# One group of small products instead of two, and a new order of a turn's parts, in the layers of a transformer on one core

## The chip, the cores and the metric

The kernel runs on one core of one Trainium2 chip. A core has five engines that matter here. TensorE (PE in the profile, PEld its weight loads) multiplies matrices, from on-chip memory into eight accumulation banks. VectorE (DVE), ScalarE (ACT) and GpSimd (POOL) do elementwise work; SyncE (SP) issues the transfers. Each engine runs its own list of instructions strictly in order, and waits, through semaphores, for what an instruction needs from other engines. So the order in which the program lists instructions on each engine decides what stands behind what.

The metric is the time of one execution on the device, in microseconds (us).

## The reference

The input x has 2 sequences of 1024 tokens with 128 features. Eight blocks follow one another, each of them adding to x: windowed attention, an expert network, causal attention, the expert network again, an attention with 16 heads, then `L1_ffn`, another attention, and `L1_ffn` once more. The change touches `L1_ffn` alone, which runs twice. It has six layers:

```python
for i in range(DEPTH):                                    # 6
    x = attn_layer(shift_tokens(x), Wqkv[i], q_scale[i], k_scale[i], Wo[i]) + x
    x = ffn_layer(shift_tokens(x), ln_g[i], ln_b[i], W1[i], b1[i], W2[i], b2[i]) + x
```

`attn_layer` makes queries, keys and values for 16 heads of 64 numbers, scales queries and keys to length one (`l2norm`), rotates them by position, and lets each window of 32 tokens attend to itself and to the window before: products of queries and keys, a mask, a softmax, products with the values, and a projection back to 128 features. `ffn_layer` normalises each token, makes 2 x 341 numbers of it, multiplies one half by the gelu of the other, and goes back to 128 features.

## The kernel before, in words

Class `Layers` works on tiles of 128 tokens (four windows). A layer has 2 x 8 tiles, a call 6 x 16 = 96, numbered m. The tile stays in on-chip memory from layer to layer. The work on one tile is cut into some 70 steps, each a method of the class that issues a few instructions. The attention steps come once a tile, the `ffn_...`, `gate...` and `value...` steps (the list `BY_BLOCK`) once in four tiles, on 512 tokens at a time.

The steps are software-pipelined by hand. `ORDER` is a list of words such as `scores0:0`; `turns` goes through it once a turn, and in turn n the word `step:late` runs that step for tile m = n - late. So a step with late -3 works three tiles ahead of one with late 0. The place in the list sets the order in which the instructions of one turn stand on each engine's list; nothing rearranges them afterwards (`manual_schedule`). A call has 110 turns, the first ones and the last ones only partly filled.

A tile passes through these steps. The numbers after a step's name are its arguments; for queries and keys the first is s (0 queries, 1 keys), the second the half u.

- `project` s u (L1448, PE): queries or keys of 128 tokens, 512 columns, into one bank of the pool `pj` (four banks).
- `squares` s u (L1457, ACT) reads that bank and squares it; `rotate` s u (L1477, DVE) reads the same bank and multiplies by the rotary table into `t1` and `t2`, of which there are two buffers each.
- `halves` s (L1483, POOL) adds the two halves of the squares; `lengths` s (L1489, DVE) sums them per head; `inverses` (L1502 to L1504, ACT) makes one over the root.
- `join` s (L1494, POOL) adds `t1` and `t2` into `raw`; `scale` s (L1509, POOL) multiplies `raw` by the inverse lengths.
- `flip` s c (L201, PE, tile `tqk`): four transposes into one of two banks of tag `tp`; `heads` s c (L1527, ACT) copies them out. `carry` (L1542, POOL) hands the last keys on to the next tile.
- `project_v` r (L1550, PE), `values` r (L1559, ACT), `windows` r (L1567 to L1574, SP): values, and eight transfers that lay them out by window.
- `scores` (L1588 and L1597, PE): eight mask matmuls and 64 small products, of 64 x 32 by 64 columns, which PE runs several at a time in parts of its array. The profile counts each product as two matmuls, for a float32 product takes two passes. `below_max` j (DVE), `exps` j (ACT) and `sums` (DVE) are the softmax.
- `flip_p` j (PE, tile `tpr`), `probabilities` j (ACT); `outputs` (L1647, PE): 64 small products again; `divide` r (DVE).
- `flip_o` r (PE, tile `to`), `features` r (ACT), `project_out` (L1679, PE: 16 matmuls in the profile), `add_out` (DVE).
- for four tiles: `ffn_flip`, `ffn_stats`, `ffn_dev`, `ffn_norm`, `ffn_back`, `ffn_gain`, three `gate_in` and `gate`, three `value_in` and `value`, `ffn_out` (L1789), `ffn_add`.

Before, `scores` and `outputs` each come in two parts, `scores0` and `scores1`, `outputs0` and `outputs1`, with half of the small products each (64 matmuls of the profile), and other PE work between the parts. Weights and rotary tables are fetched inside `project`, `rotate` and `ffn_add`, whichever of a layer's calls comes first.

Of the kernel before, what the change touches and what calls it, by code (L numbers as in the profile page):

```python
# [11 lines left out]
F32 = mybir.dt.float32  # L12
# [6 lines left out]
P = 128  # L19
# [11 lines left out]
DEPTH, LH, LD, LW = 6, 16, 64, 32  # L31
# [1019 lines left out]
class Experts:  # L1051
# [223 lines left out]


ORDER = """
    value_in1:11 halves0:-2 join0:-2 add_out:3 flip11:0 divide0:2 divide1:2 project_v0:0 ffn_flip:7
    heads01:0 flip_p0:1 gate_in0:9 heads11:0 value_in0:11 lengths1:-1 value1:11 value_in2:10 values0:0
    scores0:0 lengths0:-2 inverses:-1 project10:-2 ffn_back:8 flip_p1:1 ffn_stats:7 gate0:9 value0:11  # L1280
    ffn_out:11 ffn_dev:7 squares10:-2 sums:1 ffn_norm:7 project11:-2 carry:0 project00:-3 value2:10
    rotate10:-2 scores1:0 probabilities0:1 squares11:-2 project_v1:0 ffn_gain:8 probabilities1:1
    flip_o0:2 scale1:-1 ffn_add:11 gate_in2:9 flip_o1:2 windows0:0 rotate11:-2 squares00:-3 values1:0
    scale0:-1 gate_in1:9 rotate00:-3 features0:2 features1:2 below_max0:0 halves1:-2 gate2:9
    below_max1:0 project01:-3 flip10:-1 gate1:9 squares01:-3 exps0:0 outputs0:1 join1:-2 heads10:-1
    rotate01:-3 project_out:2 flip00:-1 heads00:-1 exps1:0 outputs1:1 flip01:-1 windows1:0
"""
BY_BLOCK = (
    "ffn_flip", "ffn_stats", "ffn_dev", "ffn_norm", "ffn_back", "ffn_gain", "gate_in", "gate",
# [4 lines left out]
class Layers:  # L1294
# [281 lines left out]

    def scores(self, m, part):
        nc, st = self.nc, self.get(m)  # L1580
        key = self.name(m)
        if part == 0:
            st["sc"] = [self.ps.tile([P, 8, 64], F32, tag="big", name=f"sc_{key}_{j}") for j in range(2)]
            first = self.place(m)[2] == 0
            for c in range(4):
                for j in range(2):
                    rows = slice(64 * j, 64 * j + 64)
                    nc.tensor.matmul(  # L1588
                        st["sc"][j][ts(c, 32)].rearrange("p h k -> p (h k)"), self.identb[rows, :],
                        self.wide[rows, 1 if first and c == 0 else 0, :], start=True, stop=False,  # L1590
                    )
        sc = st["sc"]
        for hp in range(4 * part, 4 * part + 4):
            for c in range(4):
                for j in range(2):
                    rows = slice(64 * j, 64 * j + 64)
                    nc.tensor.matmul(  # L1597
                        sc[j][ts(c, 32), hp, :], st["q"][rows, hp, ts(c, 32)],
                        st["k"][rows, hp, ds(32 * c, 64)], start=False, stop=(hp == 7),
                    )  # L1600
# [33 lines left out]
        pt = st["pT", j] = self.sp.tile([P, 4, P], F32, tag="pT", name=f"pT_{self.name(m)}_{j}", bufs=4)  # L1634
        self.nc.scalar.copy(pt, st["tpr", j])

    def outputs(self, m, part):
        nc, st, key = self.nc, self.get(m), self.name(m)
        if part == 0:
            st["av"] = [self.pj.tile([P, 4, 2, LD], F32, tag="pj", name=f"av_{key}_{r}") for r in range(2)]  # L1640
        av = st["av"]
        for q in range(2 * part, 2 * part + 2):
            for j in range(2):
                for c in range(4):
                    for r in range(2):
                        rows = slice(64 * r, 64 * r + 64)
                        nc.tensor.matmul(  # L1647
                            av[r][ts(c, 32), q, j, :], st["pT", j][rows, q, ts(c, 32)],
                            st["vw"][rows, c, ts(2 * q + j, LD)], start=True, stop=True,
                        )  # L1650
# [318 lines left out]
```

## Time and profile before

| | |
|---|---|
| median of three runs | 3995.49 us (3991.46 to 3996.87) |
| the profiled execution: its span | 3987.0 us |
| the median less that span | 8.5 us |
| PE busy | 3825.6 us, 96% of the span |
| DVE, ACT, POOL busy | 3116.1, 2414.0, 2535.5 us |
| mean granted clock of PE | 0.970 |
| first call of `Layers` | about 563 to 2225 us of the span |
| second call of `Layers` | about 2311 to 3973 us |
| longest waits of ACT and POOL | ACT on flips of queries 387.8, on projections 367.6; POOL on squares 308.7 us |
| PE's wait for `scale` (tqk on raw, L1509) | 13.9 us |

The profile is one execution of the program. The profiled execution's own time is known as its span, from the first to the last instruction; what a run takes beyond it is the difference in the table. A row of a group gives the line, engine, operation, output and inputs with their shapes and count, then after the bar the busy time in us and the mean length of one in ns, and after the second bar the engine's idle time just before, with what ended it. A row of a timeline gives the start and the length in us, and in brackets the idle time before it. Matmuls overlap, so on PE the difference between two starts says more than a length. The chain of work that ended last lies on PE for 87% of the span.

### The profile page before, as it was taken

The numbers are of one execution on the slowest core, as the hardware profiler recorded it, in microseconds if no ns is written. First come the engines' busy times: TensorE is split into PE (matmuls) and PEld (weight loads), VectorE is DVE, ScalarE is ACT, GpSimd is POOL, SyncE is SP. The second block draws the span as 40 slices with busy tenths as digits, with TensorE's granted clock in tenths as the row PEclk, the third lists the DMA queues.
The fourth block names the chain that finished last, engine by engine and source line by source line (L and its number), as shares of the span: only waits on it lengthen the run. The fifth ranks groups of instructions, "written<-read, shape, count | busy, mean of one in ns | idle before, by whom it ended". The sixth has DMA issues, their size and how long they took to land.

```text
span 3987.0 us, 156275 instructions
## 1 busy us (share of the span) xinstructions
PE 3825.6 (96%) x67372; PEld 2521.5 (63%) x67372; DVE 3116.1 (78%) x6012; ACT 2414.0 (61%) x4582; POOL 2535.5 (64%) x1638
## 2 busy tenths in 40 slices
PE   7898979999999999999999779999999999999998
PEld 5646436666666666666666446666666666666665
DVE  7775877778787878787887667887878787878786
ACT  3444437766666666666666458666666666666665
POOL 4541448776766667767675467766767767666662
PEclk8899979999999999999999779999999999999999
DMA  3030313232333333323222033333333323332222
GB/s 87 2 85 8 79 62 75 67 92 69 78 84 75 78 78 73 88 72 77 63 70 67 9 95 70 75 85 75 86 71 73 92 68 77 85 76 67 66 68 54
DMA packets 217397, 281.11 MB, mean 71 GB/s; under 512 B 52493, under 2 KB 108682, under 8 KB 216586
## 3 DMA queue, kind: packets, MB, share of 16 engines
q1 hardware_dynamic: 216714, 271.12, 27.9%
q8 instruction: 536, 8.78, 1.0%
q14 instruction: 147, 1.20, 0.1%
HBM read 69.46 MB, written 3.28 MB: 18 GB/s over the span
## 4 chain that ended last, share of the span: by engine, by line
PE 87%; DVE 6%; DMA 2%; POOL 2%; ACT 1%; issue 1%; SPq 0%; DVEq 0%; POOLq 0%; ACTq 0%
PE pj_l L1448 17%; PE y_l L1679 9%; PE pv_l L1550 9%; PE tqk_l L201 9%; PE av_l L1647 8%; PE sc_l L1597 7%; PE tpr_l L201 4%; PE to_l L201 4%; PE fg_l L1753 3%; PE fy_l L1789 3%; PE fa_l L1774 3%; PE sc_l L1588 2%; DMA f0share_e<-f0d_e 1%; PE f0S_e L1239 1%; DVE t_l L1477 1%
## 5 line engine op out<-in xcount | busy, mean ns | idle before, releaser
L1477 DVE TENSOR_TENSOR t_l<-pj_l,rot_l 128x512 f32<-128x512 f32 x1536 | 968.1, 684 | 368.6 <-ACT sq_l L1457 356.6
L1494 POOL TENSOR_TENSOR raw_l<-t_l,t_l 128x1024 f32<-128x1024 f32 x384 | 907.8, 2364 | 532.5 <-DVE on_l L1655 285.0
L1448 PE MATMUL pj_l<-wqkv_l,x_l 128*128 128x512 f32 x1536 | 785.9, 614 | 6.5 <-DVE t_l L1477 4.2
L1509 POOL TENSOR_TENSOR raw_l<-raw_l,rn_l 128x1024 f32<-128x1024 f32 x384 | 723.2, 1902 | 94.6 <-ACT rn_l L1504 87.4
L1483 POOL TENSOR_TENSOR sq_l<-sq_l 128x512 f32<-128x512 f32 x384 | 490.8, 1278 | 311.8 <-ACT sq_l L1457 308.7
L1457 ACT ACTIVATE sq_l<-pj_l 128x512 f32<-128x512 f32 x768 | 461.5, 603 | 369.6 <-PE pj_l L1448 367.6
L201 PE MATMUL tqk_l<-ident_sb,raw_l 128*128 128x128 f32 x3072 | 452.7, 278 | 15.5 <-POOL raw_l L1509 13.9
L1527 ACT COPY qT_l<-tqk_l 128x512 f32<-128x512 f32 x384 | 224.8, 585 | 387.9 <-PE tqk_l L201 387.8
L201 PEld LDWEIGHTS tqk_l<-ident_sb,raw_l 128*128 128x128 f32 x3072 | 356.4, 142 | 160.7 <-issue 121.3
L1550 PE MATMUL pv_l<-wqkv_l,x_l 128*128 128x512 f32 x768 | 416.4, 624 | 6.1 <-DVE ln_xn_fl L1733 5.3
L1679 PE MATMUL y_l<-outT_l,wo_l 128*128 128x128 f32 x3072 | 393.7, 281 | 0.0
L1597 PEld LDWEIGHTS sc_l<-kT_l,qT_l 64*32 64x32 f32 x24576 | 295.4, 105 | 155.5 <-issue 145.1
L1679 PEld LDWEIGHTS y_l<-outT_l,wo_l 128*128 128x128 f32 x3072 | 357.5, 191 | 18.3 <-issue 1.0
L1448 PEld LDWEIGHTS pj_l<-wqkv_l,x_l 128*128 128x128 f32 x1536 | 256.3, 192 | 172.1 <-issue 111.2
L1647 PE MATMUL av_l<-vw_l,pT_l 64*32 64x64 f32 x24576 | 360.5, 224 | 2.1 <-issue 1.7
L1559 ACT COPY v_l<-pv_l 128x512 f32<-128x512 f32 x384 | 225.1, 586 | 225.4 <-PE pv_l L1550 205.5
L1655 DVE TENSOR_TENSOR on_l<-av_l,inv_l 128x512 f32<-128x512 f32 x384 | 247.4, 686 | 121.5 <-PE av_l L1647 121.3
L1647 PEld LDWEIGHTS av_l<-vw_l,pT_l 64*32 64x32 f32 x24576 | 294.2, 105 | 70.0 <-issue 63.6
L1597 PE MATMUL sc_l<-kT_l,qT_l 64*32 64x64 f32 x24576 | 329.8, 223 | 0.3 <-issue 0.3
L201 PEld LDWEIGHTS tpr_l<-ident_sb,pr_l 128*128 128x128 f32 x1536 | 189.1, 141 | 152.3 <-issue 116.8
L1607 DVE TENSOR_TENSOR pr_l<-sc_l,mx_l 128x512 f32<-128x512 f32 x384 | 265.6, 692 | 13.2
L201 PEld LDWEIGHTS to_l<-ident_sb,on_l 128*128 128x128 f32 x1536 | 183.2, 141 | 128.4 <-issue 110.9
(317 smaller groups left out, 6208.9 us busy)
## 6 DMA issues: line engine op xcount, KB each, us to landing
vw_l<-v_l SPq DMA_DIRECT2D x3024, 64.0 KB
wqkv_l<-in_Wqkv SPq DMA_DIRECT2D x36, 512.0 KB
f0share_e<-f0d_e SPq DMA_DIRECT2D x64, 256.0 KB
rot_l<-in_rotary SPq DMA_DIRECT2D x24, 512.0 KB
wo_l<-in_Wo SPq DMA_DIRECT2D x12, 512.0 KB
w_l<-in_W SPq DMA_DIRECT2D x12, 341.0 KB
a0rows<-a0both SPq DMA_DIRECT2D x4, 512.0 KB
a0qk<-a0rows SPq DMA_DIRECT2D x32, 64.0 KB
```

The lines of the kernel that those rows point to most:

```text
L201: self.nc.tensor.transpose(tp[:, c, :], src(c), self.ident)
L1448: self.nc.tensor.matmul(pj.rearrange("p h d -> p (h d)"), self.x[b][0][:, ts(a, P)], self.w[i]["qkv"][:, ds(INNER * s + 512 * u, 512)], st ...
L1457: self.nc.scalar.activation(st["sq", s][:, u], st["pj", s, u], AF.Square)
L1477: self.nc.vector.tensor_tensor(to, st["pj", s, u], tabs[:, k, None, ts(w, LD // 2)].to_broadcast(half), ALU.mult)
L1483: self.nc.gpsimd.tensor_tensor(sq[:, 0], sq[:, 0], sq[:, 1], ALU.add)
L1494: self.nc.gpsimd.tensor_tensor(r.rearrange("p h u d -> p u h d"), st["t1", s], st["t2", s], ALU.add)
L1509: self.nc.gpsimd.tensor_tensor(r, r, st["rn"][:, ts(s, LH), None].to_broadcast([P, LH, LD]), ALU.mult)
L1550: self.nc.tensor.matmul(pj, self.x[b][0][:, ts(a, P)], self.w[i]["qkv"][:, ds(2 * INNER + 512 * r, 512)], start=True, stop=True,)
L1597: nc.tensor.matmul(sc[j][ts(c, 32), hp, :], st["q"][rows, hp, ts(c, 32)], st["k"][rows, hp, ds(32 * c, 64)], start=False, stop=(hp == 7),)
L1607: nc.vector.tensor_tensor(p, st["sc"][j], mx[:, :, None].to_broadcast([P, 8, 64]), ALU.subtract)
L1647: nc.tensor.matmul(av[r][ts(c, 32), q, j, :], st["pT", j][rows, q, ts(c, 32)], st["vw"][rows, c, ts(2 * q + j, LD)], start=True, stop=True,)
L1679: self.nc.tensor.matmul(y[:, 0:P], self.w[i]["o"][:, c, :], st["o"][:, c, :], start=(c == 0), stop=(c == 7))
```

## The change

Three edits in `Layers`:

- `scores` loses its argument `part`: the eight mask matmuls and all 64 small products stand together, 128 matmuls of small products in the profile's count.
- `outputs` loses it too.
- `ORDER` is a new list, with one word `scores` and one word `outputs`. Nearly every step has another place in the turn, and many another lateness.

The numbers of instructions on the engines stay the same. In the new list `squares` stands before `rotate` for the half 10, and behind it for 11, 00 and 01.

```diff
 ORDER = """
-    value_in1:11 halves0:-2 join0:-2 add_out:3 flip11:0 divide0:2 divide1:2 project_v0:0 ffn_flip:7
-    heads01:0 flip_p0:1 gate_in0:9 heads11:0 value_in0:11 lengths1:-1 value1:11 value_in2:10 values0:0
-    scores0:0 lengths0:-2 inverses:-1 project10:-2 ffn_back:8 flip_p1:1 ffn_stats:7 gate0:9 value0:11
-    ffn_out:11 ffn_dev:7 squares10:-2 sums:1 ffn_norm:7 project11:-2 carry:0 project00:-3 value2:10
-    rotate10:-2 scores1:0 probabilities0:1 squares11:-2 project_v1:0 ffn_gain:8 probabilities1:1
-    flip_o0:2 scale1:-1 ffn_add:11 gate_in2:9 flip_o1:2 windows0:0 rotate11:-2 squares00:-3 values1:0
-    scale0:-1 gate_in1:9 rotate00:-3 features0:2 features1:2 below_max0:0 halves1:-2 gate2:9
-    below_max1:0 project01:-3 flip10:-1 gate1:9 squares01:-3 exps0:0 outputs0:1 join1:-2 heads10:-1
-    rotate01:-3 project_out:2 flip00:-1 heads00:-1 exps1:0 outputs1:1 flip01:-1 windows1:0
+    project10:-3 ffn_add:11 value1:10 join1:-2 flip_p1:0 inverses:-2 project11:-3 squares10:-3
+    project_v0:-1 rotate10:-3 flip_p0:0 probabilities1:0 project_v1:-1 ffn_flip:6 rotate11:-3 sums:0
+    values0:-1 ffn_stats:6 gate_in0:8 squares11:-3 probabilities0:0 value_in0:10 gate_in2:8
+    flip_o0:1 value0:10 values1:-1 features0:1 project00:-4 windows0:-1 halves1:-3 join0:-3
+    flip_o1:1 features1:1 scale0:-2 gate0:8 gate2:8 ffn_dev:6 project01:-4 rotate00:-4 ffn_norm:6
+    rotate01:-4 ffn_back:7 scores:-1 flip00:-2 squares00:-4 flip01:-2 squares01:-4 scale1:-2
+    gate_in1:8 windows1:-1 heads00:-2 halves0:-4 project_out:1 heads01:-2 below_max0:-1 ffn_gain:7
+    below_max1:-1 lengths1:-3 add_out:1 outputs:0 gate1:8 flip11:-2 flip10:-2 ffn_out:10 value_in1:9
+    carry:-1 divide0:0 exps1:-1 lengths0:-4 value_in2:8 divide1:0 exps0:-1 value2:8 heads11:-2
+    heads10:-2
 """
-    def scores(self, m, part):
+    def scores(self, m):
...
-        for hp in range(4 * part, 4 * part + 4):
+        for hp in range(8):
             for c in range(4):
                 for j in range(2):
-    def outputs(self, m, part):
+    def outputs(self, m):
...
-        for q in range(2 * part, 2 * part + 2):
+        for q in range(4):
```

More of the change, by code (lines that the diff above doesn't have):

```diff
@@ L1574, in windows @@
                 nc.sync.dma_start(to, self.get(m - 1)["v"][96:128, r, :])
-    def scores(self, m, part):
+    def scores(self, m):
         nc, st = self.nc, self.get(m)
         key = self.name(m)
[L1582 to L1592, printed above, removed]
-        for hp in range(4 * part, 4 * part + 4):
+        sc = st["sc"] = [self.ps.tile([P, 8, 64], F32, tag="big", name=f"sc_{key}_{j}") for j in range(2)]
+        first = self.place(m)[2] == 0
+        for c in range(4):
+            for j in range(2):
+                rows = slice(64 * j, 64 * j + 64)
+                nc.tensor.matmul(
+                    sc[j][ts(c, 32)].rearrange("p h k -> p (h k)"), self.identb[rows, :],
+                    self.wide[rows, 1 if first and c == 0 else 0, :], start=True, stop=False,
+                )
+        for hp in range(8):
             for c in range(4):
@@ L1635, in probabilities @@
         self.nc.scalar.copy(pt, st["tpr", j])
-    def outputs(self, m, part):
+    def outputs(self, m):
         nc, st, key = self.nc, self.get(m), self.name(m)
-        if part == 0:
-            st["av"] = [self.pj.tile([P, 4, 2, LD], F32, tag="pj", name=f"av_{key}_{r}") for r in range(2)]
-        av = st["av"]
-        for q in range(2 * part, 2 * part + 2):
+        av = st["av"] = [self.pj.tile([P, 4, 2, LD], F32, tag="pj", name=f"av_{key}_{r}") for r in range(2)]
+        for q in range(4):
             for j in range(2):
```

## The prediction

> **What bounds the kernel now.** I read the engines' totals first, then the busy time per stage, the matrix engine's timeline over one turn, and the timelines and group rows of the work that feeds it. Totals and two group rows:
>
> ```profile
> PE 3825.6 (96%) x67372; PEld 2521.5 (63%) x67372; DVE 3116.1 (78%) x6012; ACT 2414.0 (61%) x4582; POOL 2535.5 (64%) x1638
> ...
> L1494 POOL TENSOR_TENSOR raw_l<-t_l,t_l 128x1024 f32<-128x1024 f32 x384 | 907.8, 2364 | 532.5 <-DVE on_l L1655 285.0
> ...
> L1509 POOL TENSOR_TENSOR raw_l<-raw_l,rn_l 128x1024 f32<-128x1024 f32 x384 | 723.2, 1902 | 94.6 <-ACT rn_l L1504 87.4
> ```
>
> A stage view of 774.50 to 2123.10 us (columns: length, then busy time of PE, PEld, DVE, ACT, POOL):
>
> ```profile
> 774.50:2123.10 1348.60, 1347.26 (x26442) 907.62 (x26441) 1084.96 (x2021) 864.17 (x1681) 941.11 (x591) 1.00 0.31 76
> ```
>
> PE is busy for 99.9% of it: inside the layers nothing but PE sets the pace. That stretch holds 20 blocks of four turns (it runs from one ffn_out, 774.51, to another, 2123.14): 67.43 us a block. Before any ffn work has started, the mask matmuls of successive turns begin at 642.60, 657.50 and 672.48: 14.93 us a turn. The PE timeline (start, length, work) shows what small products cost beside their own time:
>
> ```profile
> 1053.18 2.05 PE L1679 MATMUL y_l<-outT_l,wo_l 128*128 128x128 f32 x16
> 1055.07 0.60 PE L201 MATMUL tqk_l<-ident_sb,raw_l 128*128 128x128 f32 x4
> 1055.60 0.86 PE L1647 MATMUL av_l<-vw_l,pT_l 64*32 64x64 f32 x64
> 1056.39 1.09 PE L201 MATMUL tqk_l<-ident_sb,raw_l 128*128 128x128 f32 x8
> 1057.32 1.02 PE L1550 MATMUL pv_l<-wqkv_l,x_l 128*128 128x512 f32 x2
> 1058.18 0.60 PE L201 MATMUL tpr_l<-ident_sb,pr_l 128*128 128x128 f32 x4
> 1058.71 0.41 PE L1588 MATMUL sc_l<-wide_l,identb_l 64*32 64x512 bf16 x8
> 1058.94 0.84 PE L1597 MATMUL sc_l<-kT_l,qT_l 64*32 64x64 f32 x64
> ```
>
> Starts, not lengths, count. A projection takes 0.86 (1057.32 to 1058.18). A flip takes 0.44, but 0.53 when small products follow (1055.07 to 1055.60): entering costs 0.09. Leaving costs 0.06 to 0.10 (eight flips after outputs 0.93 instead of 0.87). So a group of small products costs about 0.19 beyond its products (0.77 to 0.79 per 64).
>
> The hand-offs, from the timeline of all engines, two places:
>
> ```profile
> 605.48 1.89 POOL L1509 TENSOR_TENSOR raw_l<-raw_l,rn_l 128x1024 f32<-128x1024 f32 x1
> ...
> 607.42 0.66 PE L201 MATMUL tqk_l<-ident_sb,raw_l 128*128 128x128 f32 x4 [0.30 <-POOL raw_l L1509]
> ```
>
> ```profile
> 1047.47 0.60 ACT L1457 ACTIVATE sq_l<-pj_l 128x512 f32<-128x512 f32 x1 [2.74 <-PE pj_l L1448]
> ...
> 1048.15 1.28 POOL L1483 TENSOR_TENSOR sq_l<-sq_l 128x512 f32<-128x512 f32 x1 [0.71 <-ACT sq_l L1457]
> 1048.16 2.48 DVE L1477 TENSOR_TENSOR t_l<-pj_l,rot_l 128x512 f32<-128x512 f32 x4
> ...
> 1061.55 1.88 PE L1448 MATMUL pj_l<-wqkv_l,x_l 128*128 128x512 f32 x4
> ...
> 1062.61 0.60 ACT L1457 ACTIVATE sq_l<-pj_l 128x512 f32<-128x512 f32 x1 [0.60 <-PE pj_l L1448]
> ...
> 1063.24 1.29 DVE L1477 TENSOR_TENSOR t_l<-pj_l,rot_l 128x512 f32<-128x512 f32 x2 [0.38 <-ACT sq_l L1457]
> ```
>
> Projection to its square 1.06 (1061.55 to 1062.61); square to rotate 0.63: DVE and ACT, both only reading the projection, take turns in their emitted order. Two rotates 2.48; square to halves 0.68; scale to flip 0.05.
>
> **The change, part by part.**
>
> *Merged groups.* No instruction goes away; per turn two of four groups do: 2 x 0.19 = 0.38 of PE. The trace has no group of 128; it lies between no gain (the first outputs group often takes 0.15 longer) and 0.38. I take 0.38, as two of the rows above joined.
>
> *The new order: the key point.* In a turn PE now does project10, flip_p1, project11, project_v0, flip_p0, project_v1, flip_o0, project00, flip_o1, project01, scores, and then flip00. That is 6 x 0.86 + 4 x 0.44 + 0.09 + 0.23 + 2 x 0.77 + 0.10 = 8.86 us until flip00 could start. But flip00 needs scale0 of its tile, and POOL issues, in order, join1, halves1, join0, scale0, scale1, halves0, carry. halves1 needs squares11 of **this** turn; squares11 now stands behind rotate11 (its reader of the same bank), which stands behind rotate10, behind squares10, behind project10. So within one turn, from project10's start to flip00's:
>
> A = 1.06 (project10 to squares10) + 0.63 (squares10) + 2.52 (rotate10, rotate11, hand-off to ACT 0.04) + 0.68 (squares11) + 1.28 (halves1) + 2.36 (join0) + 1.90 (scale0) + 0.05 = 10.48 us.
>
> PE must wait 10.48 - 8.86 = 1.6 us before flip00. The hand-off from rotate to square does not occur before; bounds are 0.03 (DVE's subtraction to ACT's exponential, 609.59 to 609.62) and 0.20 (PE to ACT); I take the near end, also DVE to ACT. Before, the scale of a tile was issued ahead of the turn's halves1 and join1, so PE waited on POOL for 13.9 us in the whole run.
>
> After flip00 the turn still has flip00 and flip01 0.87, project_out 1.79 (1.89 less leaving), 0.09, outputs 1.56, 0.10, flip11 and flip10 0.87: B = 5.28. Adding up the old turn from the same rows gives 14.54 against 14.67 to 14.93 measured, so rows run short; a third of that falls in B: + 0.1. A turn is thus L = 10.48 + 5.38 = 15.86. Where flip10 stands right before the next project10, ACT must first do heads10 (0.20 to 0.79 after project10's start) and inverses (0.95), so squares10 starts at 1.74 instead of 1.06: L' = 16.54.
>
> *ffn parts.* Those ahead of flip00 (gate_in0, gate_in2; ffn_flip, value_in0; ffn_back) fill the wait; those behind it add: gate_in1 and value_in2 1.72, value_in1 0.86, ffn_out 2.58 = 5.16 a block. One turn in four follows a turn that ends in flip10. Block: 4 x 15.86 + 0.68 + 5.16 = 69.3, + 1.9 on 67.43.
>
> *The rest.* rotate00 needs join0's buffer and now waits about 2.5 us on POOL; queued behind it on DVE are rotate01 and below_max; behind those wait exps and heads on ACT. DVE has 13.6 us of work a turn (1084.96 over 80 turns of the stage) in 16 to 18, and exps of a turn are used at the next turn's flip_p: hidden, and if not, flip_p waits up to 0.5. windows (16 transfers a turn on SP) still leads outputs by one turn. The rotary tables are fetched a turn earlier, and their multiply (2.36 on POOL, 12 times a call) now stands between scale0 and scale1: flip11 comes 4.4 after flip00, scale1 would be ready at 1.90 + 2.36 = 4.3: hidden, at worst 12 x 0.3. load_layer is a turn earlier; load_ffn keeps 20 us until gate_in0. Neither shows. The start has one more turn, the drain one less: between -16 and +16 a call, one L; I take +5, since a starting turn is pure latency.
>
> **Sum.** Per call: 21 blocks x 1.9 = 40, 9 turns without ffn parts x (16.54 - 14.93) = 14.5, + 5: 60. Two calls: + 120. The profiled execution has a span of 3987.0; the runs' median of 3995.49 lies 8.5 above it, which I keep: 4115 us. PE's wait for scale: (0.6 + 1.6 + 0.3 + 1.2) x 21 + 9 x 2.3 = 99 a call, about 200 in all.
>
> *A rule weighed: the clock.* Where PE idled in the trace, the granted clock (the figure after the POOL count) sometimes halved for the next 3.41 us. Three stretches of the stage view:
>
> ```profile
> 203.64:207.05 3.41, 1.58 (x5) 0.57 (x4) 1.39 (x2) 0.00 (x0) 0.25 (x1) 1.00 0.94 276
> ...
> 606.41:609.82 3.41, 1.44 (x7) 0.49 (x6) 3.38 (x7) 0.79 (x2) 3.41 (x4) 1.00 0.33 76
> 609.82:613.23 3.41, 3.41 (x13) 2.70 (x14) 2.85 (x5) 2.98 (x6) 3.41 (x2) 0.50 0.34 78
> ```
>
> After 1.44 us of work the next stretch had 0.50; after 1.58, from 207.05 on, 1.00. A wait of 1.6 to 2.3 leaves 1.1 to 1.8: on the edge. About 100 waits are that long (21 + 21 + 9 a call); each drop loses at most half of 3.41 = 1.7, so 0 to 170 us. [...]
>
> **The rivals.**
>
> *Clock drops (slower still).* A third of 100 waits at 1.7: + 57, 4172. For it: the row at 606.41. Against: the one at 203.64, and ffn work shortens half the waits.
>
> *PE stays the bound (faster).* If the chain to scale0 is in fact shorter, the wait goes: 192 x 0.38 = 73 less, 3922. It decides at + 120 us / (2 x 93 turns) = 0.65 a turn, so at A below 9.8. For it: POOL rows are rough, PE is 99.9% busy. Against: halves1, join0 and scale0 alone are 5.54, and they can't start before the second square.
>
> *squares11 isn't held by rotate11 (no real change).* ACT would reach it after values0, at 3.7, instead of 4.21: A = 9.97, 120 - 186 x 0.51 = + 25, 4020. Against: the row at 1063.24, where such a reader waited.
>
> **How the numbers follow.** Forecast 0.60 (own range 4060 to 4170: the start +-32, B +-20, hand-offs + 30), clock drops 0.24, no hold 0.06, PE bound 0.10. A kernel of this spread can tell 0.2%, 8 us, from no change. Faster 0.10; of the no-hold case and the forecast's low edge 0.04 land within 8 us; slower 0.86. The range of 4025 to 4215 leaves out the PE bound (0.10) and the heavier half of the clock drops.
>
> **What would show it.** PE busy falls to about 92%; PE's wait of tqk on POOL raw (the scale line) rises from 13.9 to about 200; POOL waits some 5 us a turn on ACT's square; rotates wait on POOL; block 69.3. Wrong if that PE wait stays under 100, or if the granted clock falls below 0.95 in the layers.

## The result and the profile after

The changed kernel takes 4220.34 us (median of four runs, 4219.36 to 4225.73), the kernel before 3995.64: 1.0573 times as long, 95% interval 1.0558 to 1.0588. It is slower by 225 us where 120 was forecast, 5 us beyond the upper end of the range. The profiled execution has a span of 4223.9 us, 237 more than that of before.

The engines' totals of the changed kernel, with three of its groups:

```profile
PE 3749.2 (89%) x67372; PEld 2527.7 (60%) x67372; DVE 3113.5 (74%) x6012; ACT 2405.1 (57%) x4582; POOL 2508.9 (59%) x1638
...
L1484 POOL TENSOR_TENSOR sq_l<-sq_l 128x512 f32<-128x512 f32 x384 | 489.1, 1274 | 1196.9 <-ACT sq_l L1458 1194.9
...
L1495 POOL TENSOR_TENSOR raw_l<-t_l,t_l 128x1024 f32<-128x1024 f32 x384 | 908.8, 2367 | 0.0
...
L1510 POOL TENSOR_TENSOR raw_l<-raw_l,rn_l 128x1024 f32<-128x1024 f32 x384 | 724.1, 1906 | 11.5 <-ACT rn_l L1505 11.5
```

Two rows of the kernel before, to compare:

```profile
L1483 POOL TENSOR_TENSOR sq_l<-sq_l 128x512 f32<-128x512 f32 x384 | 490.8, 1278 | 311.8 <-ACT sq_l L1457 308.7
...
L1647 PE MATMUL av_l<-vw_l,pT_l 64*32 64x64 f32 x24576 | 360.5, 224 | 2.1 <-issue 1.7
```

PE is busy 76 us less than before (3825.6) and yet the program is longer: PE no longer sets the pace. POOL waits 1195 us for squares (309 before). The chain of work that ended last, 87% of it on PE before, is now spread over the engines:

```profile
PE 41%; POOL 27%; DVE 17%; ACT 9%; issue 4%; DMA 2%; SPq 0%; ACTq 0%; POOLq 0%; DVEq 0%
```

The waits of PE (us in total, times, longest):

```profile
PE tqk_l L201 <- POOL raw_l L1510: 232.9, 192, 10.6
PE av_l L1644 <- issue: 35.0, 25, 2.4
...
PE tqk_l L201 <- issue: 12.7, 12, 2.5
```

The first is the wait for scale, 13.9 before. The other two are new in this size: PE stands still inside or just behind a group of outputs and waits for nothing that the profile shows ("issue"). Before, this was 1.7 us at the outputs.

One turn of the changed kernel, from the timeline of all engines. It is the chain that the prediction added up:

```profile
1199.45 1.02 PE L1449 MATMUL pj_l<-wqkv_l,x_l 128*128 128x512 f32 x2
...
1200.57 0.60 ACT L1458 ACTIVATE sq_l<-pj_l 128x512 f32<-128x512 f32 x1 [1.97 <-PE pj_l L1449]
...
1201.27 2.49 DVE L1478 TENSOR_TENSOR t_l<-pj_l,rot_l 128x512 f32<-128x512 f32 x4
1203.79 0.60 ACT L1458 ACTIVATE sq_l<-pj_l 128x512 f32<-128x512 f32 x1 [0.54 <-DVE t_l L1478]
...
1204.53 1.27 POOL L1484 TENSOR_TENSOR sq_l<-sq_l 128x512 f32<-128x512 f32 x1 [6.32 <-ACT sq_l L1458]
...
1205.76 2.37 POOL L1495 TENSOR_TENSOR raw_l<-t_l,t_l 128x1024 f32<-128x1024 f32 x1
1208.07 3.78 POOL L1510 TENSOR_TENSOR raw_l<-raw_l,rn_l 128x1024 f32<-128x1024 f32 x2
...
1210.04 1.09 PE L201 MATMUL tqk_l<-ident_sb,raw_l 128*128 128x128 f32 x8 [1.37 <-POOL raw_l L1510]
```

From project10 at 1199.45 over squares10, the two rotates, squares11, halves1, join0 and scale0 to flip00 at 1210.04 are 10.59 us (forecast 10.48); POOL idles 6.32 before halves1. The next projection starts at 1215.19: a turn of 15.74 (forecast 15.86). In 159 turns of the blocks the first of these stretches has a median of 10.58, and half of the turns have 10.58 to 10.94. So the mechanism was there at its forecast size, and the missing 105 us lie elsewhere. The mask matmuls of scores come once a turn; their starts divide the two calls:

| stretch, both calls together | forecast, us | after less before, us |
|---|---|---|
| up to the first scores of each call, and the end of the program | 10 | 23.1 + 21.2 - 2.8 = 41.5 |
| the nine turns from there (ffn work begins in the seventh) | 29 | 42.23 + 43.33 = 85.6 |
| the next 80 turns, 20 blocks of four | 76 | 55.0 + 51.6 = 106.6 |
| the last six turns | 0 to 4 | 3.3 |
| sum | 115 to 119 | 237 |

(237 is the difference of two profiled executions; 12 of it is how these stand to the medians.) Two of the rows, the filling turns and the blocks, are what the experiments take apart. The kernel before had medians of 3995.7, 3990.8 and 3994.1 us beside the three sets of them; each ratio is taken to its own set, and a difference across sets is good to some 5 us. The parts of the program ahead of the first call of `Layers`, which no experiment edits, differ as well: its first projection starts at 562.9 us before, at 565.8 in the changed kernel, and at 563.6 to 574.5 in the experiments. So what an edit did is safer to read from its own stretch than from a few us of the whole time.

### The profile page after: what moved, and what is told of

Read it like the earlier page. It is cut to its first block, busy times and chain, and to the rows that moved or that the text cites. A ratio compares the mean times of both kernels' runs of the same rounds, so it can differ in the third digit from the quotient of the medians.

```text
span 4223.9 us, 156245 instructions
## 1 busy us (share of the span) xinstructions
PE 3749.2 (89%) x67372; PEld 2527.7 (60%) x67372; DVE 3113.5 (74%) x6012; ACT 2405.1 (57%) x4582; POOL 2508.9 (59%) x1638
## 3 DMA queue, kind: packets, MB, share of 16 engines
q8 instruction: 535, 8.77, 0.9%
## 4 chain that ended last, share of the span: by engine, by line
PE 41%; POOL 27%; DVE 17%; ACT 9%; issue 4%; DMA 2%; SPq 0%; ACTq 0%; POOLq 0%; DVEq 0%
DVE t_l L1478 12%; POOL raw_l L1495 11%; PE tqk_l L201 9%; POOL raw_l L1510 8%; PE y_l L1676 8%; PE av_l L1644 7%; POOL sq_l L1484 6%; ACT sq_l L1458 5%; PE fy_l L1786 3%; PE pj_l L1449 3%; PE fa_l L1771 2%; ACT kT_l L1528 1%; PE fg_l L1750 1%; DMA f0share_e<-f0d_e 1%; PE f0F_e L1239 1%
## 5 line engine op out<-in xcount | busy, mean ns | idle before, releaser
L1478 DVE TENSOR_TENSOR t_l<-pj_l,rot_l 128x512 f32<-128x512 f32 x1536 | 958.3, 684 | 682.6 <-POOL raw_l L1495 459.1
L1484 POOL TENSOR_TENSOR sq_l<-sq_l 128x512 f32<-128x512 f32 x384 | 489.1, 1274 | 1196.9 <-ACT sq_l L1458 1194.9
L1449 PE MATMUL pj_l<-wqkv_l,x_l 128*128 128x512 f32 x1536 | 807.7, 610 | 21.8 <-ACT sq_l L1458 9.0
L201 PE MATMUL tqk_l<-ident_sb,raw_l 128*128 128x128 f32 x3072 | 436.8, 286 | 248.2 <-POOL raw_l L1510 232.9
L1551 PE MATMUL pv_l<-wqkv_l,x_l 128*128 128x512 f32 x768 | 392.4, 593 | 0.0
L1676 PEld LDWEIGHTS y_l<-outT_l,wo_l 128*128 128x128 f32 x3072 | 375.9, 198 | 23.6 <-issue 12.5
L1644 PE MATMUL av_l<-vw_l,pT_l 64*32 64x64 f32 x24576 | 300.5, 226 | 35.0 <-issue 35.0
L1652 DVE TENSOR_TENSOR on_l<-av_l,inv_l 128x512 f32<-128x512 f32 x384 | 262.9, 686 | 77.7 <-PE av_l L1644 72.9
L1596 PE MATMUL sc_l<-kT_l,qT_l 64*32 64x64 f32 x24576 | 313.2, 225 | 2.9 <-issue 2.6
L201 PEld LDWEIGHTS tpr_l<-ident_sb,pr_l 128*128 128x128 f32 x1536 | 193.0, 142 | 203.7 <-issue 165.9
L1644 PEld LDWEIGHTS av_l<-vw_l,pT_l 64*32 64x32 f32 x24576 | 263.7, 105 | 60.6 <-issue 36.4
L1610 ACT ACTIVATE pr_l<-pr_l 128x512 f32<-128x512 f32 x384 | 221.0, 623 | 126.8 <-DVE pr_l L1606 126.4
L1528 ACT COPY kT_l<-tqk_l 128x512 f32<-128x512 f32 x384 | 206.4, 587 | 146.4 <-PE tqk_l L201 142.6
```

The costliest lines, as they stand in the source:

```text
L201: self.nc.tensor.transpose(tp[:, c, :], src(c), self.ident)
L1449: self.nc.tensor.matmul(pj.rearrange("p h d -> p (h d)"), self.x[b][0][:, ts(a, P)], self.w[i]["qkv"][:, ds(INNER * s + 512 * u, 512)], st ...
L1478: self.nc.vector.tensor_tensor(to, st["pj", s, u], tabs[:, k, None, ts(w, LD // 2)].to_broadcast(half), ALU.mult)
L1484: self.nc.gpsimd.tensor_tensor(sq[:, 0], sq[:, 0], sq[:, 1], ALU.add)
L1551: self.nc.tensor.matmul(pj, self.x[b][0][:, ts(a, P)], self.w[i]["qkv"][:, ds(2 * INNER + 512 * r, 512)], start=True, stop=True,)
L1596: nc.tensor.matmul(sc[j][ts(c, 32), hp, :], st["q"][rows, hp, ts(c, 32)], st["k"][rows, hp, ds(32 * c, 64)], start=False, stop=(hp == 7),)
```

## The experiments

First, which of the two edits costs the time. "Merge alone" keeps the old list:

```diff
-    scores0:0 ... scores1:0 ... outputs0:1 ... outputs1:1
+    scores:0  ...           ...            ... outputs:1
```

> The list of before with one word scores at the place of scores0 and one word outputs at the place of outputs1. Theory (PE set the pace before, and a group switch costs 0.19): two of four groups a turn go, 2 x 0.19 x 192 turns = 73 us less, about 3923 (3915 to 3940); PE busy about 3753, its share of the span still 95% or more. Rival (a group of 128 makes PE run out of instructions, as the waits of 1.0 to 2.5 us inside the groups of the changed kernel suggest, about one in eight turns): 24 x 1.5 = 36 us come back, about 3960, and the waits of PE on 'issue' at the products of outputs come up in the groups view. Second rival (the outputs a little earlier or the scores earlier against their inputs make PE wait): 3995 or more, with a wait of PE on ACT, DVE or a DMA in its place.

Measured: 3951.33 us, 0.9889 (0.9874 to 0.9905) of before: 44 us less, not 73. Its waits of PE:

```profile
PE av_l L1643 <- issue: 19.7, 24, 2.0
...
PE sc_l L1595 <- issue: 13.6, 19, 1.5
...
PE tqk_l L201 <- issue: 8.5, 11, 1.9
```

Merging helps, and it brings 42 us of waits on "issue" with it. The first rival's 3960 was nearer than the theory's 3923.

"Order alone" keeps the new list and the groups of 64:

```diff
+    scores0:-1 project01:-4 rotate00:-4 ... rotate01:-4 ffn_back:7 scores1:-1 flip00:-2
+    ... heads00:-2 halves0:-4 outputs0:0 project_out:1 ... add_out:1 outputs1:0
```

> The new list with scores and outputs in two parts each: scores0 ahead of project01, scores1 at the place of scores; outputs0 ahead of project_out, outputs1 at the place of outputs. Theory (the chain from project10 over rotate11, squares11, halves1, join0 and scale0 sets the turn): the split scores lie inside PE's wait and cost nothing, the split outputs lie behind flip00 and cost 0.19 x 192 = 36 us: about 4255 (4240 to 4265), PE's wait for scale falls from 233 to about 195, and the waits of PE on 'issue' inside the groups stay. Rival (those waits come from groups of 128): 24 x 1.5 = 36 us less, about 4220, and those waits are gone. Rival (the merge, not the order, made the kernel slower): 4000 to 4100.

Measured: 4249.12 us, 1.0632 (1.0614 to 1.0649). So the order costs 253 us, and in this order the merge brings 29. PE's wait for scale is 196.1 us, as expected. The theory was wrong on one point: the waits on "issue" at outputs fell from 35.0 to 7.5 us and at the flips from 12.7 to 0.9. They belong to the groups of 128, not to the order. That did not bring the rival's 4220: by the starts of the mask matmuls the 20 blocks of both calls are 11 us longer than in the changed kernel, so that the switches of the split groups took more than those waits gave (PE is busy for 3852.3 us, 103 more than in the changed kernel), and 14 us of the 29 lie between the two calls, where neither edit works.

Next, what in the order makes PE wait. One word of the changed kernel is moved:

```diff
-    project_v0:-1 rotate10:-3 ... project_v1:-1 ffn_flip:6 rotate11:-3 sums:0
-    values0:-1 ffn_stats:6 gate_in0:8 squares11:-3
+    project_v0:-1 rotate10:-3 ... project_v1:-1 ffn_flip:6 squares11:-3 rotate11:-3 sums:0
+    values0:-1 ffn_stats:6 gate_in0:8
```

> One word of the changed kernel moved: squares11 stands right before rotate11, so that ACT squares the bank before DVE rotates it. Theory (squares11 is held by rotate11, and that makes the chain longer than PE's own work): squares11 starts at about 2.4 instead of 4.2 after project10, scale0 is done at 2.4 + 0.68 + 1.28 + 2.36 + 1.90 = 8.6, below PE's own 8.86: PE's wait for scale falls from 233 to under 60 us, a block of four turns to about 65.9 (67.4 of before less 4 x 0.38), the nine filling turns of a call to about 17; 4220 - 2 x (21 x 4.3 + 9 x 2) = about 4000 (3970 to 4030). Rival (squares11 not held: ACT comes to it late anyway): at most 0.5 a turn, 186 x 0.5 = 93, 4130 or more. Rival (what costs is PE out of instructions or the clock): the wait goes but waits on 'issue' grow, 4100 or more.

Measured: 4024.80 us, 1.0073 (1.0052 to 1.0093) of before: 196 us less than the changed kernel (4220), by the place of one word. The same part of a turn, in its timeline:

```profile
1201.01 1.02 PE L1449 MATMUL pj_l<-wqkv_l,x_l 128*128 128x512 f32 x2
...
1202.13 0.60 ACT L1458 ACTIVATE sq_l<-pj_l 128x512 f32<-128x512 f32 x1 [0.26 <-PE pj_l L1449]
...
1203.37 0.60 ACT L1458 ACTIVATE sq_l<-pj_l 128x512 f32<-128x512 f32 x1 [0.16 <-PE pj_l L1449]
...
1204.10 1.28 POOL L1484 TENSOR_TENSOR sq_l<-sq_l 128x512 f32<-128x512 f32 x1 [3.83 <-ACT sq_l L1458]
```

The second square starts 2.36 us after project10 (4.34 in the changed kernel), both scales are done at 1211.4 and flip00 starts with no wait on POOL: the wait for scale over the run is 35.1 us. The rival "squares11 isn't held" falls by the rows of the changed kernel: in each of the 159 turns ACT stood idle before squares11 (0.54 us, median) until a rotate ended. But the word moved past `values0` too, which ACT did ahead of squares11 before: of the 1.98 us that squares11 gained in the turn shown, the hold is 0.54, and the rest is its place behind the work of `values0`. The 196 us belong to both together; no run separates them. The time is 25 us above the expected 4000. Waits on "issue" are 63 us here, 13 more than in the changed kernel; what makes up the other 12 was not taken apart.

The other place where the chain can be cut is POOL's list:

```diff
-    project00:-4 windows0:-1 halves1:-3 join0:-3 flip_o1:1 features1:1 scale0:-2
+    project00:-4 windows0:-1 scale0:-2 halves1:-3 join0:-3 flip_o1:1 features1:1
```

> One word of the changed kernel moved: scale0 stands ahead of halves1 and join0 on POOL, so that flip00 no longer waits for the turn's own squares11. Squares11 stays behind rotate11. Theory (it is POOL's list, squares11 to halves1 to join0 to scale0, that carries the wait): PE's wait for scale falls from 233 to under 60, a steady block to about 66.5, and the filling turns to about 16, since the table loads then only delay POOL's scale, which has time: 4220 - 2 x (21 x 3.8 + 9 x 3) = about 4005 (3960 to 4060). Rival (the late join0 passes its lateness on to rotate00, squares00 and the banks of the projections): a wait of PE on ACT or DVE for a projection bank takes its place, 4100 or more. Rival (the order costs something else): 4200.

Measured: 4109.81 us, 1.0284 (1.0247 to 1.0320). The wait for scale is gone (13.9 us), and a block without stops of PE is 16.2 + 15.6 + 16.4 + 17.2 = 65.4 us. But the first seven filling turns stay at 17.6 to 20.3 us: POOL's scale now waits for the inverses (349.4 us over the run), and at the first ffn part of the first call PE waits 2.18 us for a bank that a late rotate still holds. The waits on "issue" are 82 us. So the chain to scale can be cut at POOL too, as the theory had it, but 105 us of the expected gain stayed out. The time is the first rival's; its cause is not shown, for PE's waits for a projection bank are 10.5 us on rotates and 9.0 on squares, against 7.8 and 9.0 in the changed kernel.

Then the filling turns. They mostly take 18.8 us in the first call and 20.4 in the second, where 16.54 was forecast. ACT's timeline of one of them (changed kernel):

```profile
733.41 0.33 ACT L1503 ACTIVATE rn_l<-ss_l,least_l 128x32 f32<-128x32 f32 x1
733.77 1.28 ACT L1504 ACT_TABLE_LOAD   x1
735.06 0.32 ACT L1504 ACTIVATE rn_l<-rn_l,least_l 128x32 f32<-128x32 f32 x1
735.40 1.28 ACT L1505 ACT_TABLE_LOAD   x1
736.69 0.23 ACT L1505 ACTIVATE rn_l<-rn_l 128x32 f32<-128x32 f32 x1
736.83 0.58 ACT L1458 ACTIVATE sq_l<-pj_l 128x512 f32<-128x512 f32 x1
```

`inverses` loads a function table for the logarithm and another for the exponential, 1.28 us each, right before squares10. `run` asks for one table with both, but that load stands at 0.74 us of the program, long before, and other blocks load other tables after it; only the first `gate` brings it back. Until then the first ffn part of a call loads two tables more (L1723, L1724, 1283 ns each). The kernel before has the same loads, the row of the other line being alike:

```profile
L1503 ACT ACT_TABLE_LOAD x22 | 28.2, 1283 | 0.4
```

The experiment:

```diff
 def inverses(self, m):
+    if m == 0:
+        nc.scalar.preload_act_table_set(LN_EXP)
```

> The changed kernel, with ACT's function table that holds both the logarithm and the exponential loaded once, ahead of the first inverses of a call; without it the turns before the first gate load a table twice each. Theory (those two loads of 1.283 us lie on the chain heads10, inverses, squares10 of the filling turns): a filling turn falls from 18.8 to about 16.3 in the first call, and from 20.4 to 16.5 or so in the second, where the clock drops once a turn: 2.57 x 10 x 2 = 51 us less, up to 75 with the clock: 4145 to 4170. Rival (the loads are hidden, the filling turns are long because of the chain and the clock alone): less than 15 us, 4205 or more.

Measured: 4180.25 us, 1.0469 (1.0448 to 1.0490) of before: 40 us less than the changed kernel, and 10 above the theory's range. The same steps in its timeline take 0.86 us instead of 3.42, and the mask matmuls there are 16.2 us apart (708.28, 724.50, 740.77):

```profile
734.10 0.34 ACT L1505 ACTIVATE rn_l<-ss_l,least_l 128x32 f32<-128x32 f32 x1
734.47 0.32 ACT L1506 ACTIVATE rn_l<-rn_l,least_l 128x32 f32<-128x32 f32 x1
734.82 0.23 ACT L1507 ACTIVATE rn_l<-rn_l 128x32 f32<-128x32 f32 x1
734.96 0.58 ACT L1458 ACTIVATE sq_l<-pj_l 128x512 f32<-128x512 f32 x1
```

The nine turns of both calls fall by 27.5 + 32.3 = 60 us in the profiled execution, and 17 us are lost again between the calls, mostly in a block that this edit does not touch (see the end). The old list has the same loads. What they cost there:

> The kernel before, with nothing but the function table for logarithm and exponential loaded once a call. It tells how much of the 40 us that this saved in the changed kernel belongs to the change. Theory (the loads cost the old order only at the start of a call and at the first ffn parts, where the merge with spaced groups gained 22): 3970 (3962 to 3980), so that some 20 of the 40 belong to the change. Rival (hidden in the old order): 3985 or more, and all 40 belong to it. Rival (the same price in any order): 3955 or less, and none does.

Measured: 3975.93 us, 0.9957 (0.9941 to 0.9974): 18 us. Its nine turns fall by 5.5 + 7.1. So of the 40 us that the loads cost in the changed kernel, 22 come with the change; by the nine turns alone it is 60 us against 13. With both repairs in the changed kernel:

> The changed kernel with both repairs: squares11 ahead of rotate11, and the function table loaded once a call. Theory (two separate losses): a filling turn falls from 16.2 to 18 with the first repair to about 14.5, 2 x 9 x 2.3 = 40 less than 4025: 3985 (3970 to 4000); the waits of PE on 'issue', 64 us, stay. Rival (with squares11 early the table loads are hidden): 4015 or more.

Measured: 3974.20 us, 0.9951 (0.9932 to 0.9969). The filling turns are 14.2 us. The table loads cost 51 us in this order, more than the 40 expected: the loads cost no less with squares11 early, so the two losses are separate.

Then PE's waits on "issue". One of them, in PE's timeline of the changed kernel:

```profile
1192.62 1.47 PE L1644 MATMUL av_l<-vw_l,pT_l 64*32 64x64 f32 x127
1195.80 0.21 PE L1644 MATMUL av_l<-vw_l,pT_l 64*32 64x64 f32 x1 [1.71 <-issue]
```

The last product of the group comes 1.71 us late. The profile lists two queues of instructions (packets, MB, share of the engines' span). Here is the larger one over the whole run, and then in the stretch from 1193.3 to 1193.4 us, in which one of its packets starts:

```profile
q8 instruction: 535, 8.77, 0.9%
```

```profile
q8 instruction: 1, 0.02, 59.5%
```

8.77 MB in 535 packets are 16.4 KB a packet. No row says whose instructions they are. An estimate, if they are PE's: 8.77 MB for 2 x 67372 matmuls and weight loads are 65 bytes each, so a packet holds some 250, about one group of 128 products (128 matmuls and 128 loads), and PE uses them up in 1.5 us (1.47 for 127 matmuls above). In the transfer records of the changed kernel all but two of the 43 waits on "issue" above 0.25 us from the first call on end 1.0 to 1.6 us after such a packet landed, 2.2 to 2.9 us after it started; the two are at a first projection of a call. At a random time the last packet landed 0.7 to 9 us earlier in eight cases of ten, and 1.0 to 1.6 us earlier in less than one of ten. Two kernels test it. In the first the two groups of a turn stand apart, in the old order:

```diff
-    scores:0 lengths0:-2 inverses:-1 ... project00:-3 value2:10 rotate10:-2 probabilities0:1
+    lengths0:-2 inverses:-1 ... project00:-3 value2:10 rotate10:-2 scores:0 probabilities0:1
```

> As the merge alone (3951), but scores stands at the place of scores1, in the middle of the turn, so that PE has some 7 us between the end of a group of outputs and the next scores and some 5 us from there to the next outputs, where the merge alone has about 2.3 and 9. The waits of PE on 'issue' in the layers are 49 us with the merge alone. Theory (PE runs out of instructions where two groups of 128 follow each other closely, because the fetching of them falls behind): those waits fall below 15 us and the time to about 3915 (3905 to 3928). Rival (a group of 128 stalls by its length alone, wherever it stands): the waits stay near 49 and the time near 3950. Rival (the later scores make the softmax late): a wait of PE for probabilities or for the ffn parts comes up, over 3950.

Measured: 3922.33 us, 0.9814 (0.9775 to 0.9852), 29 us less than the merge alone. The waits on "issue" at scores are gone, those at the outputs and flips fall from 28.2 to 24.4 us:

```profile
PE av_l L1643 <- issue: 18.7, 17, 1.9
...
PE tqk_l L201 <- issue: 5.7, 7, 1.2
```

The distance matters, but less of the waits went than expected (42 to 24, not under 15): 24 us stay with the groups of 128 set apart. The time fell by 29 us, the waits by 18; the other 11 are not taken apart. In the second, on top of both repairs, the groups stand together:

```diff
-    ffn_back:7 scores:-1 flip00:-2 ... lengths1:-3 add_out:1 outputs:0
+    ffn_back:7 scores:-1 outputs:0 flip00:-2 ... lengths1:-3 add_out:1
```

> The changed kernel with both repairs (3974), and outputs moved to stand right behind scores: one group of 256 products (plus the masks) a turn. Its waits of PE on 'issue' are what is asked for; the time also has waits for projection banks in it, which outputs now needs earlier. Theory (PE runs out of instructions in a long group, because they arrive more slowly than small products use them up): those waits rise from 65 us to over 130, 0.7 or more a turn, and the time is 4000 or more although one more group switch is saved (0.19 x 192 = 36). Rival (those waits have another cause, and do not go with the length of the group): they stay near 65, and the time is 3940 to 3975.

Measured: 4275.35 us, 1.0713 (1.0684 to 1.0742), with 210 us of such waits:

```profile
PE av_l L1646 <- issue: 184.4, 169, 2.3
...
PE tqk_l L201 <- issue: 16.4, 11, 2.1
```

At 169 places, nearly once a turn, PE stops in the group. Of 194 waits above 0.25 us, 192 end 1.0 to 1.6 us after an instruction packet landed; the other two are again at a first projection. The waits for projection banks that the expectation names are in its time too, so the time proves less than the row.

Last, whether the order has yet another price. The new list with groups of 64 and both repairs:

> The new order with groups of 64 (as in the order alone), with both repairs: squares11 ahead of rotate11, function table loaded once. Theory (the new order costs nothing but the two losses repaired here): from 3974, two more group switches + 73 and the waits on 'issue' from 65 to about 12, - 53: 3994 (3980 to 4010). Rival (the order has a further loss of its own): 4015 or more. Rival (splitting the groups gains more than the switches cost): under 3975.

Measured: 3987.34 us, 0.9978 (0.9962 to 0.9994). It lies within the theory's range, and 11 us above the old list with the same tables. In the profiled executions (20 us apart) 8 of these lie ahead of the first call already. From the first projection to the first scores the new order loses 12.5 and 8.9 us; in the 20 blocks of both calls it wins 7, in the last six turns 10. So it has a price at the start of a call.

The version that follows from all this is the old list with the groups merged and set apart, and the table loaded once:

> The merge with spaced groups, and the function table for logarithm and exponential loaded once a call. Theory (in the old order PE sets the pace of the filling turns too, 14.0 us each, so ACT's table loads are hidden there): within 10 us of the merge with spaced groups. Rival (the loads are on the path in any order): 40 us less.

Measured: 3899.92 us, 0.9759 (0.9727 to 0.9790): 2.4% faster than before and the fastest of all. That is 22 us less than without the edit, where under 10 were expected, but not all of it is the loads'. The nine turns fall by 8.0 + 4.5 = 12.5 us, as in the kernel before (12.6); 4 of it in each call lie in the eighth turn, in which the first ffn part loads its two tables too (20.3 and 19.1 fall to 16.3 and 15.1). Another 7.4 us lie ahead of the first projection of the first call and 7.0 between the last scores of the first call and the first projection of the second, where the edit does nothing.

The way from before to after, each step between two kernels that were run: 3996 before; 3976 with the table loaded once; 3987 by the new order with both repairs; 3974 by the merge; 4025 with the table loads back; 4220 with squares11 behind rotate11 and `values0`. The last step is by far the largest.

## Why the prediction was right and wrong

**The key point** was right. A was 10.48 against 10.59 measured, L 15.86 against 15.74, PE's wait for scale 200 against 232.9, POOL's wait on squares 5 us a turn against 1194.9 / 192 = 6.2, the rotates' wait on join0 2.5 against 459.1 / 192 = 2.4. (The terms given as 8.86 add up to 8.88; nothing hangs on it.) That squares11 is held by rotate11, both only reading one bank, is in the rows, and that its place makes the chain is shown by moving one word, past `values0` too: 196 us.

**Merged groups** is one of the three steps that failed. It set the value "between no gain (...) and 0.38" and took the gain; it had no loss side, and there is one. PE's busy time fell by 76 (forecast 73), but PE stops on "issue" at the groups of 128, 50 us over the run at scores, outputs and the flips behind them. 43 of these lie in the 20 blocks of both calls; without them a block would be (106.6 - 43) / 40 = 1.6 us longer than before, where 1.9 was forecast. The old profile could have warned: it lists the same instruction queue (536 packets, 8.78 MB), and the rate of a group, by the estimate above 16.4 KB in 1.5 us, stood in it for groups half as long only. At the outputs and the flips the waits are 47.7 us with groups of 128 and 8.4 in the same order with groups of 64; with both groups together there are 210 us of such waits.

**The filling turns** failed as a term: L' counted `inverses` at 0.95 us, its length in the steady turns. Until the first gate it takes 3.42, for two table loads. The groups of the old profile show these (22 at each of two lines, 1283 ns each); before the change PE's own work hid most of them in the nine turns (12.6 us came out when they went), and the new order put `inverses` ahead of squares10 on the chain. With the loads gone a filling turn measured 16.2, so L' was right without them. In the nine turns the change costs 85.6 us; with the loads gone in both kernels it is 85.6 - 59.8 + 12.6 = 38, where 29 was forecast. In the medians the loads are less of the miss: 22 of the 105 us.

**The start of a call** failed as well. "Between -16 and +16 a call", with +5 taken as the latency of one starting turn: from the first projection to the first scores the calls take 57.3 and 58.0 us, before 37.1 and 38.8, 20 and 19 more. The drain gave nothing back (3.3 us more in the last six turns, 2.8 less behind them). PE's waits in that stretch of the first call, before (562.9 to 600.1 us):

```profile
PE tqk_l L201 <- POOL raw_l L1509: 4.5, 2, 3.8
```

and after (565.9 to 623.2):

```profile
PE tqk_l L201 <- POOL raw_l L1510: 12.8, 2, 10.6
PE pj_l L1449 <- ACT sq_l L1458: 4.9, 3, 3.7
```

So 13 of the 20 us are the first tile's wait for scale and projections that wait for squares to free their banks. With squares11 first the stretches are 51.3 and 49.5 us, with both repairs 47.6 and 50.2: about half of the loss remains, with 10.1 us of wait for scale in the first call. Which words of the list make it remain, no run took apart; that stays open.

**The rest.** The merged group's place against vw, the rotary multiply, load_layer and load_ffn, all costed at nothing, left no new row among PE's longest waits; none was tried by itself. One new row stands there that the prediction did not have: flip_o waits for the copies of `probabilities` (25.3 us in 30 waits, 1.0 before), ahead of flip00 in the turn.

**The clock** term is 0 in the sum, and no run shows that gaps of this length cost no clock: 0 held in the steady part and not in the filling turns. Stage views (length, busy times, then the granted clock), before:

```profile
565.00:800.00 235.00, 217.20 (x4034) 142.83 (x4034) 180.79 (x348) 163.75 (x294) 174.75 (x109) 0.95 0.31 79
```

and after:

```profile
565.00:800.00 235.00, 168.36 (x2822) 108.43 (x2823) 137.94 (x271) 126.79 (x225) 127.72 (x81) 0.87 0.24 64
...
800.00:2300.00 1500.00, 1390.96 (x28312) 968.37 (x28313) 1149.39 (x2142) 917.79 (x1789) 987.85 (x627) 1.00 0.30 73
```

The clock stays at 1.00 in the mean, with PE waiting for scale 86 times in that stretch, 44 of them for 1.0 to 2.2 us. In the second call it drops in seven of the nine filling turns. From the fourth to the eighth it does so once a turn, with no gap of PE longer than 1.98 us in them; here is the fifth:

```profile
2575.83:2579.25 3.42, 1.44 (x36) 1.28 (x21) 3.04 (x5) 1.06 (x2) 3.42 (x3) 0.90 0.36 83
2579.25:2582.66 3.41, 3.41 (x34) 3.29 (x41) 2.63 (x6) 2.25 (x5) 3.41 (x4) 0.60 0.25 58
```

The stretch with 1.44 us of work is followed by one at 0.60, as the row from 606.41 of before, with 1.44 us as well, was by one at 0.50. What goes with the drops here is the busy time of a stretch. Cut into the stretches of 3.41 us at whose ends the clock changes in this trace, the two calls of the changed kernel (from the first scores to the last) have 18 stretches at full clock that are followed by half the clock; PE was busy for 1.57 us or less in each. In the 945 that are followed by full clock it was busy for 1.54 us or more.

What the clock took in the filling turns can be read from PE's busy time for the same matmuls, here in the second call, first the changed kernel, then with the table loaded once:

```profile
2494.51:2675.68 181.17, 140.86 (x2761) 98.34 (x2760) 108.45 (x196) 109.57 (x195) 105.04 (x68) 0.92 0.24 55
```

```profile
2483.81:2632.66 148.85, 127.10 (x2761) 88.82 (x2760) 107.93 (x195) 83.49 (x173) 104.54 (x68) 0.98 0.29 67
```

PE's work is 13.8 us shorter, and in the first call 10.4 (137.30 and 126.89, at 0.94 and 0.99). So up to 24 of the 60 us that the nine turns fell by went with the clock, in both calls. The rival "Clock drops" came nearest in time (4172) with a cause that is the smaller part.

**The rivals** "PE stays the bound" and "squares11 isn't held" fell: A was 10.59, not under 9.8, and the hold is real.

## What to carry to other kernels

When two engines read the same bank and the second of them waits for the first, as here, put the reader first whose result other engines wait for; moving one such reader ahead gave 196 us, part of which was its place behind another step on its own engine. A step costed at its steady length must be looked up in the starting turns too, where other work (table loads here) can sit on the same lines. And a long run of very short instructions needs its own bound: compare the bytes of its instructions with the time that it lasts (here some 16.4 KB in 1.47 us, by the estimate above), and set such runs apart, which took 29 us from the merge alone.

## What the runs showed of the hardware

PE's stops on "issue" go with the packets of the instruction queue: 41 of 43 in the changed kernel, and 192 of 194 with both groups together, end 1.0 to 1.6 us after a packet of 16.4 KB landed. That PE had run out of instructions there fits these runs, and no row says it. In the changed kernel many of these stops come 140 us apart; from 1056.3 to 1195.8, eight turns, the instruction queue moved 21 packets, so that they seem to fall where the packets' boundaries meet the group in the same way again. That was not tested further.

For some turns the turn and the clock ran in step. In the second call's filling turns of the changed kernel the mask matmuls from 2553.99 to 2635.68 us are 20.4 us apart, and the granted clock drops to 0.50 five times, 20.48 us apart (2558.06 to 2639.98), six times the 3.41 us that each of these drops lasts. With the table loads gone the mask matmuls of the first call's filling turns are 16.2 us apart.

The clock between the calls differed between two kernels, though nothing was edited there. In the changed kernel with the table loaded once, the stretch from 2350 to 2400 us, between the calls, ran at a granted clock of 0.50, with PE busy for 46.6 of the 50 us; in the changed kernel the stretches from 2350 to 2400 and from 2380 to 2430 us had 0.76 and 0.74. The gap from the last scores of the first call to the first of the second grew from 187.1 to 203.7 us, which took back 17 of the 60 us that the filling turns had gained. Each of these is one profiled execution, and the four runs with the table loaded once lie 18 us apart, at mean clocks of 0.955 to 0.962, so it is not shown that the edit moved the clock.
